# A three-layer graph network on one core: end-node distances on ScalarE, scales of node tiles 8 to 15 found together

## The chip, the cores and the metric

The kernel runs on one core of a Trainium2 chip. Its engines have instruction queues of their own: TensorE (PE in the profile; PEld is its weight load), VectorE (DVE), ScalarE (ACT), GpSimd (POOL) and SyncE (SP, which here only issues DMAs). The metric is the device time of one execution in microseconds (us); the median of several runs is compared.

## The reference

2500 nodes with 256 features each, 80000 edges sorted by their end node `dst`. Each node row is normalized, put through a relu, and three edge convolutions follow; all four states go through one final product, which is added to the input.

```python
def _edge_conv(x, src, dst, W, b):
    xi = x[dst]
    xj = x[src]
    m = jnp.concatenate([xi, xj - xi], axis=-1) @ W + b
    s = jax.ops.segment_sum(m, dst, num_segments=N)
    cnt = jax.ops.segment_sum(jnp.ones((dst.shape[0],), m.dtype), dst, num_segments=N)
    return s / jnp.maximum(cnt, 1.0)[:, None]
...
h = jnp.maximum(_layernorm(x, axis=-1), 0.0)
xs = [h]
for W, b in ((W0, b0), (W1, b1), (W2, b2)):
    h = jax.nn.relu(_edge_conv(h, src, dst, W, b))
    xs.append(h)
return x + jnp.concatenate(xs, axis=-1) @ Wf + bf
```

## The kernel before

The sums over edges are done as matrix products with a matrix of edge counts between nodes. The kernel builds that matrix itself, in the first layer, and keeps a copy in DRAM for the other two. The nodes are 20 tiles of 128 (10 pairs q of two tiles each). The end nodes are cut into 417 windows of 6 nodes; 128 windows make a stretch group i, and there are four of them (0 to 3, the last with 33 windows).

What happens before about 62 us is called the head here. It has two strands of work.

**The nodes.** For each pair q: statistics `st` (line 681 on), for a group of pairs at a time the scales: `spread` adds the epsilon (`rs`, VectorE), `roots` takes the square root (ScalarE), `scales` makes the reciprocal and the offset `off` (VectorE), lines 693 to 702. Then `normalize` applies them (GpSimd for q of 2 and more, otherwise VectorE and ScalarE), `turn` transposes on TensorE, `take_turned` copies with a relu on ScalarE, and `product` makes the first layer's node product `pz` (and the final product's part). ScalarE and VectorE split the product in a high and a low part, `zh` and `zl`.

**The edges.** TensorE, ScalarE and VectorE find where in the edge list each window's edges begin (`count_half`, `search`: the numbers `start_i`). GpSimd then gathers 256 edges for each window, one window on each of the 128 partitions: `ed` from `dst`, then `es` from `src` (`get_edges`, line 584; the last group from `longer`, a copy of the edge list with an end piece). `key_parts` (line 596) makes from them `lo_i`, the low 7 bits of the source, and `away`, how far the end node lies behind the number just under the window's first node, or 0. A second instruction sets the latter half of `away` to 0 where it is small. `key_low` and `key_high` turn them into the keys `km` and `kn`; `key_turn` transposes these on TensorE, `key_copy` copies them out. `compare` (VectorE) makes the 0/1 matrices `one_m` and `one_n` from the keys, for two blocks of four windows at a time (three buffers); `counts` multiplies them on TensorE into a bank, and `take_counts` copies the bank into the count matrix `a` on ScalarE. `away` is read again later, between 62 and 108 us, for the degrees of the nodes.

Most of the instructions are made through `InOrder` wrappers (line 272), so each engine runs its part of the list exactly in the order in which it was written. For the head that order is a string of short names (line 900 on), performed from left to right: a name is a step, the digits its argument. The steps that matter here, with their engines: `st` statistics (VectorE), `rs` spread (VectorE), `sq` root (ScalarE), `sc` scales (VectorE), `N` normalize, `T` turn (TensorE), `R` take_turned (ScalarE), `Z` and `F` products (TensorE), `H` and `L` the high and low parts (ScalarE, VectorE), `G` copy of the final part (ScalarE), `pk` and `sg` counting in the edge list (TensorE, ScalarE), `se` search (VectorE), `ge` gathers (GpSimd), `ka` key_parts, `km` key_low (ScalarE), `kb` key_high (VectorE), `kt` key_turn (TensorE), `k1` and `k2` key_copy (ScalarE), `B` compare (VectorE), `C` counts (TensorE), `E` take_counts (ScalarE). So `ka2` is key_parts of stretch group 2, and `C5` the counts of block 5. The argument of `rs`, `sq` and `sc` is an index in the list `groups` (line 882).

An engine that has to wait for an operand stops there, and all that is behind it in its queue stops too.

After the head the first layer's big products run, while the rest of the count matrix is built beside them, then the other two layers and the final product.

Of the kernel before, what the change touches and what calls it, by code (L numbers as in the profile page):

```python
# [10 lines left out]
AF = mybir.ActivationFunctionType  # L11
OP = mybir.AluOpType
# [301 lines left out]
def by_windows(ctx: ExitStack, tc: tile.TileContext, x, src, dst, Ws, bs, Wf, bf, out, missing):  # L314
    nc = tc.nc
    PE, DVE, ACT, POOL, SP = nc.tensor, nc.vector, nc.scalar, nc.gpsimd, nc.sync
    PEo, DVEo, POOLo, ACTo, SPo = (InOrder(tc, e) for e in (PE, DVE, POOL, ACT, SP))
# [19 lines left out]
    N1 = NT * (W - SKIP)  # L337
# [10 lines left out]
    Q = NT // 2  # L348
# [34 lines left out]
    away = early.tile([P, WG, CAP], BF16, name="away")  # L383
# [13 lines left out]
    lim = const.tile([P, WG], F32, name="lim")  # L397
    below = const.tile([P, WG], F32, name="below")
# [135 lines left out]
    def limits():  # L534
        DVEo.tensor_copy(lim, lim_i)
        DVEo.tensor_copy(limr, limr_i)
        DVEo.tensor_scalar(below, lim, -1.0, None, op0=OP.add)
        DVEo.tensor_scalar(unlim, lim, -1.0, 0.5, op0=OP.mult, op1=OP.add)
        DVEo.tensor_scalar(after, row_i[:, 0:1], -1.0, float(2 ** 20), op0=OP.is_ge, op1=OP.mult)
        DVEo.tensor_copy(dst_r[:, :MORE], row_i)  # L540
# [55 lines left out]
    def key_parts(i):  # L596
        es, ed = edges[i]
        lo_i = pw.tile([P, CAP], I32, name="lo_i")
        DVEo.tensor_scalar(lo_i, es, P - 1, None, op0=OP.bitwise_and)

        DVEo.tensor_scalar(away[:, i, :], ed, below[:, i:i + 1], 0.0, op0=OP.subtract, op1=OP.max)
        DVEo.scalar_tensor_tensor(away[:, i, P:], away[:, i, P:], float(SKIP + 1), away[:, i, P:],
                                  op0=OP.is_ge, op1=OP.mult)
        parts[i] = [lo_i]
# [169 lines left out]
    def new_a(g):  # L774
        return apools[g % 2].tile([P, NT, GS], F32R, name="a")
# [74 lines left out]
    def layer(l, g, a, own, PE=PE, ACT=ACT):  # L850
# [28 lines left out]

    groups = [(0, 1), (1, 2), (2, 4), (4, 6), (6, 8), (8, Q)]
    a = new_a(0)
    acts = {
        "lim": limits, "first": find_first, "next": find_next, "pick": find_rows,
        "long": lengthen,
        "dstr": lambda: ACTo.copy(dst_r[:, MORE:], dst_i),
        "pk": lambda i: pick_half(i // 10, i % 10), "sg": lambda i: count_half(i // 10, i % 10),
        "se": lambda i: search(*((0, 1), (1, WG))[i]), "ge": get_edges,
        "ka": key_parts, "km": key_low, "kb": key_high, "kt": key_turn,  # L890
        "k1": lambda i: key_copy(i, 0), "k2": lambda i: key_copy(i, 1),
        "io": small_numbers, "ws": lambda: DVEo.tensor_sub(ws[0][0], ws[0][0], ws[0][1]),
# [6 lines left out]
    }  # L899
    order = """  # L900
        long warm8 lim io first next dstr st0 rs0 sq0 pick sc0 warm7 N0 pk00 sg00 pk01 st1 T0 pk11 R0 sg01 st4 rs1 sq1 Z0 pk30 se0
        sg11 sc1 pk20 N1 st5 sg30 ge0 T1 st6 R1 rs3 F0 sg20 pk21 sq3 st7 pk10 H0 F1 rs4 st3 sq4 sc4 G0 st9
        sc3 L0 sg21 N6 pk31 ka0 kb0 Z1 N5 st8 N7 G1 T6 rs5 sg10 sg31 km0 T5 se1 kt0 R6 H1 st2 F6 sq5 sc5 k10 k20
        rs2 Z6 ge1 L1 T7 B0 R5 R7 Z5 B1 C0 B2 ka1 G6 H6 N9 H5 C1 T9 F7 E0 ge2 kb1 R9 sq2 km1 E1 kt1 C2 B3 k21 Z9
        k11 N8 L6 B4 E2 L5 C3 B5 C4 T8 E3 E4 C5 V9 R8 E5 ge3 ka2 H9 sc2 Z7 H7 F8 G7 B6 N3 N2 ka3 km2 T2 R2 km3
        kb2 C6 T3 kb3 B7 L7 kt2 Z2 B8 B9 L9 E6 C7 k22 k12 kt3 H2 N4 E7 B10 k13 k23 Z8 L2 C8 T4 C9 E8
# [478 lines left out]
def gnn_kernel(tc: tile.TileContext, x, src, dst, Ws, bs, Wf, bf, out):  # L1385
    nc = tc.nc
    with tc.tile_pool(name="flag", bufs=1) as flag:
        missing = flag.tile([1, 1], I32, name="missing")
        by_windows(tc, x, src, dst, Ws, bs, Wf, bf, out, missing)
        again = nc.values_load(missing, min_val=0, max_val=1)  # L1390
        with tc.If(again > 0):
            general(tc, x, src, dst, Ws, bs, Wf, bf, out)
# [28 lines left out]
```

## Time and profile before

| | before |
|---|---|
| runs | 478.38, 478.60, 479.85 us; median 478.6 |
| profiled execution | 478.51 us, its span 476.7 us, granted TensorE clock 0.996 |
| TensorE, weight load | 465.9 us busy, 366.5 us |
| VectorE, ScalarE, GpSimd | 375.0, 302.1, 41.6 us busy |

The head in stretches of 12 us (busy time of each engine in it):

| stretch, us | PE | DVE | ACT | POOL |
|---|---|---|---|---|
| 0 to 12 | 9.40 | 10.08 | 6.26 | 3.73 |
| 12 to 24 | 11.47 | 11.68 | 8.33 | 7.47 |
| 24 to 36 | 11.45 | 10.47 | 8.70 | 10.66 |
| 36 to 48 | 11.08 | 11.00 | 7.81 | 2.10 |
| 48 to 60 | 12.00 | 11.47 | 7.10 | 0.00 |

Most rows of this kernel carry the line L282, that of the wrapper which records every operation, so its groups are told apart by the tiles that they write and read. A row `away<-ed,below 128x256 bf16<-128x256 int32` writes `away` from `ed` and `below`. A row's length can overlap the next row's start on the same engine, since instructions are pipelined; the distance from one start to the next is then what it takes of the engine. The four instructions `away<-ed,below` take 0.34 to 0.58 us on VectorE in the page's times, mean 0.46; the four casts `km<-lo_i` of the same shape on ScalarE 0.40.

### The profile page before, as it was taken

The page shows a single profiled execution, that of the slowest core. Times are in us where ns is not written, and L with a number is a line of the kernel's source. Part 1 is how long each engine was busy: PE and PEld are TensorE (multiplying, and loading weights), DVE is VectorE, ACT ScalarE, POOL GpSimd, SP SyncE. Part 2 cuts the span into 40 slices and gives each one's busy share as a digit, 9 for nine tenths or more (in the row PEclk, how much of TensorE's full clock was granted, in tenths as well). Part 3 has the DMA queues.
Part 4 walks back from the last instruction along what each step waited for, and adds up shares of the span by engine and source line. Part 5 has one row for each costly group of instructions (what it writes and reads, how often), then busy time and mean ns, then how long its engine had stood idle before and what let it go on. Part 6 is the DMA issues. An engine that isn't in the chain of part 4 may idle for free.

```text
span 476.7 us, 7301 instructions
## 1 busy us (share of the span) xinstructions
PE 465.9 (98%) x2723; PEld 366.5 (77%) x2723; DVE 375.0 (79%) x687; ACT 302.1 (63%) x527; POOL 41.6 (9%) x66
## 2 busy tenths in 40 slices
PE   7999999999999999999999999999999999999994
PEld 4887888777777778878887877876788788688694
DVE  8988987987788874649987847877899687569785
ACT  5776576664554435067778866874787798497540
POOL 3681015200100101000000000000000000000000
PEclk9999999999999999999999999999999999999998
DMA  9310078990550905522268551110213955220033
GB/s 285 112 53 4 1 156 162 192 214 9 102 118 1 203 16 101 119 89 52 79 188 321 210 174 27 61 43 2 87 43 90 356 185 175 87 88 0 0 98 124
DMA packets 21845, 52.73 MB, mean 111 GB/s; under 512 B 1977, under 2 KB 12170, under 8 KB 21770
## 3 DMA queue, kind: packets, MB, share of 16 engines
q1 hardware_dynamic: 14730, 34.31, 21.2%
q0 software_dynamic: 5856, 16.51, 18.2%
q10 hardware_dynamic: 1216, 1.37, 0.9%
q8 instruction: 23, 0.38, 0.3%
q14 instruction: 20, 0.16, 0.1%
HBM read 36.72 MB, written 16.10 MB: 111 GB/s over the span
## 4 chain that ended last, share of the span: by engine, by line
PE 87%; DVE 7%; DMA 2%; POOL 2%; issue 1%; SPq 0%; DVEq 0%
PE bank L282 85%; PE pz L282 2%; DMA acc<-in_x_dram 1%; DVE st L282 1%; DVE acc L282 1%; POOL acc L282 1%; DVE one_m L282 1%; DVE staged L282 1%; DMA es<-longer,start_i 1%; POOL ed L282 1%; DVE one_n L282 1%; DVE zl L282 0%; DVE away L282 0%; DVE mv L282 0%; POOL es L282 0%
## 5 line engine op out<-in xcount | busy, mean ns | idle before, releaser
L282 ACT CAST block<-staged 128x1008 fp32r<-128x1008 bf16 x120 | 117.8, 1031 | 16.9 <-DVE staged L282 6.3
L282 ACT CAST a<-bank 128x480 fp32r<-128x480 f32 (+1 forms) x105 | 52.9, 565 | 60.7 <-PE bank L282 60.7
L282 PE MATMUL bank<-a,zh 128*128 128x504 f32 (+1 forms) x200 | 84.4, 422 | 0.0
L282 PE MATMUL bank<-block,zh 128*128 128x504 f32 (+1 forms) x200 | 83.8, 419 | 0.0
L282 DVE TENSOR_TENSOR one_m<-iota_m,key_m 128x2048 bf16<-128x2048 bf16 (+2 forms) x55 | 64.3, 1169 | 21.4 <-PE bank L282 21.3
L282 PE MATMUL bank<-a,zl 128*128 128x504 f32 (+1 forms) x200 | 77.9, 389 | 0.0
L282 PE MATMUL bank<-block,zl 128*128 128x504 f32 (+1 forms) x200 | 77.4, 387 | 0.0
L282 PE MATMUL bank<-block,sh 128*128 128x504 f32 x160 | 69.1, 432 | 0.0
L282 PE MATMUL bank<-block,staged 128*128 128x512 f32 (+1 forms) x312 | 66.5, 365 | 0.3 <-DVE staged L282 0.3
L282 PE MATMUL bank<-block,sl 128*128 128x504 f32 x160 | 62.7, 392 | 0.0
L282 PEld LDWEIGHTS bank<-block,staged 128*128 128x128 f32 x312 | 52.5, 188 | 10.7 <-issue 0.7
L282 DVE TENSOR_TENSOR one_n<-iota_n,key_n 128x960 bf16<-128x960 bf16 (+2 forms) x110 | 55.5, 545 | 0.0
L282 DVE TENSOR_TENSOR block<-staged 128x1008 fp32r<-128x1008 bf16 x40 | 46.9, 1205 | 5.5 <-PE bank L282 4.3
L282 PEld LDWEIGHTS <-one_m 128*128 128x128 bf16 x834 | 39.1, 98 | 11.2 <-issue 7.2
L282 PEld LDWEIGHTS bank<-a,zh 128*128 128x128 f32 x200 | 37.8, 189 | 10.7 <-issue 2.6
L282 PEld LDWEIGHTS bank<-block,zh 128*128 128x128 f32 x200 | 37.6, 188 | 10.8 <-issue 2.5
L282 PEld LDWEIGHTS bank<-block,zl 128*128 128x128 f32 x200 | 37.6, 188 | 10.5 <-issue 3.2
L282 PE MATMUL bank<-one_n,one_m 128*128 128x120 bf16 x834 | 44.5, 209 | 1.1 <-DVE one_n L282 1.0
L282 PEld LDWEIGHTS bank<-a,zl 128*128 128x128 f32 x200 | 37.8, 189 | 8.9 <-issue 2.6
L282 DVE TENSOR_TENSOR staged<-staged 128x1008 bf16<-128x1008 bf16 x40 | 27.1, 679 | 17.3 <-ACT block L282 16.9
L282 PE MATMUL pz<-wbf,hT 128*128 128x256 f32 x160 | 38.6, 387 | 0.7 <-DMA wbf<-in_L_gnn_Wf_dram 0.4
L282 PEld LDWEIGHTS bank<-block,sh 128*128 128x128 f32 x160 | 30.1, 188 | 10.4 <-issue 3.5
(155 smaller groups left out, 591.1 us busy)
## 6 DMA issues: line engine op xcount, KB each, us to landing
staged<-a_dram SPq DMA_DIRECT2D x52, 504.0 KB, 4.0
a_dram<-a POOLq DMA_DIRECT2D x20, 630.0 KB, 8.6
out_dram<-acc SPq DMA_DIRECT2D x17, 128.0 KB, 1.8
acc<-in_x_dram POOLq DMA_DIRECT2D x3, 640.0 KB, 13.1
wbf<-in_L_gnn_Wf_dram SPq DMA_DIRECT2D x4, 256.0 KB, 6.9
acc<-in_x_dram SPq DMA_DIRECT2D x1, 896.0 KB, 9.4
acc<-in_x_dram ACTq DMA_DIRECT2D x1, 768.0 KB, 6.9
wbf<-in_L_gnn_W_dram SPq DMA_DIRECT2D x3, 256.0 KB
```

Source lines behind the costliest of these rows:

```text
L282: return self.tc.keep_in_program_order(call(*args, **kwargs))
```

## The change

The distance `away` is made by one ScalarE instruction, relu(`ed` + `below`), in place of one VectorE instruction, max(`ed` - `below`, 0); `below` has the opposite sign for it. The masking of the latter half stays on VectorE. In `groups`, the pairs 4, 5 and 6, 7 become one entry, so the scales of their tiles 8 to 15 are made in one step; its `rs` and `sq` stand at the place that those of the pairs 6, 7 had, and one step each of `rs`, `sq` and `sc` is gone. The entry after it has the index 4 in place of 5.

```diff
     def limits():
...
-        DVEo.tensor_scalar(below, lim, -1.0, None, op0=OP.add)
+        DVEo.tensor_scalar(below, lim, -1.0, 1.0, op0=OP.mult, op1=OP.add)
...
     def key_parts(i):
...
-        DVEo.tensor_scalar(away[:, i, :], ed, below[:, i:i + 1], 0.0, op0=OP.subtract, op1=OP.max)
+        ACTo.activation(away[:, i, :], ed, AF.Relu, bias=below[:, i:i + 1])
         DVEo.scalar_tensor_tensor(away[:, i, P:], away[:, i, P:], float(SKIP + 1), away[:, i, P:],
                                   op0=OP.is_ge, op1=OP.mult)
...
-    groups = [(0, 1), (1, 2), (2, 4), (4, 6), (6, 8), (8, Q)]
+    groups = [(0, 1), (1, 2), (2, 4), (4, 8), (8, Q)]
...
-        sg11 sc1 pk20 N1 st5 sg30 ge0 T1 st6 R1 rs3 F0 sg20 pk21 sq3 st7 pk10 H0 F1 rs4 st3 sq4 sc4 G0 st9
-        sc3 L0 sg21 N6 pk31 ka0 kb0 Z1 N5 st8 N7 G1 T6 rs5 sg10 sg31 km0 T5 se1 kt0 R6 H1 st2 F6 sq5 sc5 k10 k20
+        sg11 sc1 pk20 N1 st5 sg30 ge0 T1 st6 R1 F0 sg20 pk21 st7 pk10 H0 F1 rs3 st3 sq3 sc3 G0 st9
+        L0 sg21 N6 pk31 ka0 kb0 Z1 N5 st8 N7 G1 T6 rs4 sg10 sg31 km0 T5 se1 kt0 R6 H1 st2 F6 sq4 sc4 k10 k20
```

## The prediction

> **What bounds the kernel now.** I read the page first: TensorE is busy nearly all of the span, and the table of waits shows it waiting hardly at all after 62 us (0.3 us, for a staged block). So only the head can give or cost time, and only through moments in which TensorE waits there.
>
> ```profile
> PE 465.9 (98%) x2723; PEld 366.5 (77%) x2723; DVE 375.0 (79%) x687; ACT 302.1 (63%) x527; POOL 41.6 (9%) x66
> ```
>
> Next the chain of waits (start, length, what), which shows what carries the head:
>
> ```profile
> 16.91 0.34 DVE lo_i L282
> 17.25 0.50 DVE away L282
> ...
> 33.37 3.43 DMA es<-longer,start_i
> ...
> 36.90 0.29 DVE lo_i L282
> 37.19 0.50 DVE away L282
> ...
> 47.26 0.49 DVE one_n L282
> 47.75 0.04 issue
> 47.80 0.81 PE bank L282 x15
> ```
>
> VectorE carries it from the first statistics on, GpSimd and its last gather (`es` of stretch group 3) for some 13 us, VectorE again to 47.75; from 47.80 it is TensorE, without a break to the end of the head. Two of the four `away` instructions that the change removes stand on this chain. What TensorE loses shows in its own timeline (start, length; in brackets the idle time before and its releaser):
>
> ```profile
> 32.85 0.23 PE L282 MATMUL bank<-one_n,one_m 128*128 128x120 bf16 x1 [0.38 <-DVE one_n L282]
> 33.25 0.46 PE L282 MATMUL bank<-one_n,one_m 128*128 128x80 bf16 x7 [0.17 <-DVE one_n L282]
> 33.55 3.69 PE L282 MATMUL pz<-wbf,hT 128*128 128x256 f32 x16
> 37.08 0.60 PE L282 MATMUL turned<-shift,acc 128*128 128x128 f32 x4
> ...
> 38.96 0.29 PE L282 MATMUL bank<-ident_b,kn 128*128 128x128 bf16 x2 [0.35 <-DVE kn L282]
> 39.08 1.95 PE L282 MATMUL pz<-wbf,hT 128*128 128x256 f32 x8
> 41.33 0.23 PE L282 MATMUL bank<-one_n,one_m 128*128 128x120 bf16 x1 [0.30 <-DVE one_n L282]
> 41.73 0.46 PE L282 MATMUL bank<-one_n,one_m 128*128 128x80 bf16 x7 [0.17 <-DVE one_n L282]
> ```
>
> These are C5, the products Z7 and F8, T2, the turning kt2 of the keys, Z2 and C7. The named idle times sum to 1.4 us; a further 0.4 us or so follows before 47.80 (C11). By starts of one kind of work (C5 could start 32.3, when T8 is issued) the loss is about 0.9 at C5, 0.6 at kt2, 0.5 at C7. About 2 us is all that a faster VectorE can give, 0.4% of the time.
>
> **The groups edit, costed at nothing.** Gone are one `rs` add (0.07 of VectorE's time), one square root on ScalarE (0.11 to the next start), one reciprocal and one `off` (15.87 to 16.29: 0.33 with their gaps): 0.4 us on VectorE before 16.9. But the `lo_i` at 16.91 needs `es` of group 0: that gather is issued at 12.59 and lands 4.3 later, at 16.89. In before, the subtraction `zl` ends at 16.90, so the landing is hidden to the last 0.02; in after VectorE comes at 16.5 and waits until 16.9. The start of that gather (POOL, behind `start_i` at 10.64) is not touched. Moving the root later costs nothing: it follows H0 on ScalarE, ends near 14.45 as the old second root did (14.32 + 0.23), before VectorE wants it at 14.7. Node group N6 on GpSimd waits for the same reciprocal as before (15.19). Folding the sign into `below` changes no count.
>
> **The `away` edit: what VectorE saves.** Four instructions go. From start to the next start they take 0.50 (17.25), 0.37 (26.47 to 26.84), 0.38 (33.65) and 0.53 (37.19 to 37.72). What must come in time is ScalarE's replacement.
>
> *Its price.* No row of before has Relu of integers with a bias. Nearest from below: the cast `km<-lo_i`, same shape and types, 0.40. From above: Relu over `away`, 128x256 with a bias operand, 0.50. The Trainium skill (ScalarE: Activation LUTs, What ACT_TABLE_LOAD costs) gives 280 ns + 0.833 ns an element with such a bias, which for 256 is an estimate of 0.49; I take 0.50, 0.40 from one start to the next. The same page (Rules for kernel authors) speaks against the edit: relu and add belong on VectorE. By that rule four instructions of 0.46 mean are exchanged for four of 0.50: 0.2 us lost if both engines counted alike. By the rows, ScalarE has gaps and VectorE none from 8.4 to 34.6, so the sum is kept by place. A table load has no reason: Relu and Sqrt already alternate here behind the one load at 1.69.
>
> *Place 0.* ScalarE reaches it at 16.16, after the read of the last count, and then sat idle 0.91 before G1 at 17.17, waiting for TensorE. `ed` landed at 11.10 + 4.8 = 15.9. So it ends at 16.66, before `lo_i` ends at 17.25: nothing waits, and VectorE gains 0.50. `se1` then comes at 19.6; its last count is read at 18.92.
>
> *Place 1.* ScalarE comes at 24.82, behind R7; `ed` lands at 21.0 + 2.8 = 23.8 or earlier. G6, H6 shift by 0.40, of which the 0.16 idle and the overlap before H5 absorb all but 0.1; then E0 and R9 have 0.1. TensorE sees none. VectorE's gain is 0.87 by B3 (27.71 becomes 26.84).
>
> *Place 2: here the edit adds a real wait.* On ScalarE it stands behind E5, and E5 waits for C5 on TensorE. C5 now starts at 32.3 and ends 32.85; R8 (32.60) lets E5 start at 33.09; `away` runs 33.55 to 34.05. VectorE would have come at 32.8 and stands still until 34.09; its masking ran at 34.03 before. So the 0.87 is lost again at this point. Behind it wait `sc2`, then N3 and N2 on GpSimd (34.71, released by `off`; nodes 4 and 5 ready at 36.9 as before), and T2 on TensorE. TensorE, 0.9 early out of C5, idles some 0.7 at T2; from T2's second half at 37.05 it is 0.25 early, and reaches kt2 at 38.1 and Z2 at 38.3 if the keys are there.
>
> *Place 3: what the gain rests on.* VectorE was idle 2.29 before 36.90, for the last gather; it decides again. GpSimd's timeline, with its two slow gathers:
>
> ```profile
> 27.94 1.82 POOL L282 DMA_INDIRECT es<-in_src_dram,start_i  x1 [0.30 <-issue]
> 31.05 2.02 POOL L282 DMA_INDIRECT ed<-longer,start_i  x1 [0.16 <-issue]
> 34.71 3.40 POOL L282 TENSOR_SCALAR acc<-acc,rs,off 128x256 f32<-128x256 f32 x6 [0.37 <-DVE off L282]
> ```
>
> The first two started inside a `one_m` of VectorE (begun 27.71 and 31.01), and end 0.92 after it gives way to `one_n` (28.84, 32.15); undisturbed gathers take 0.96. The Trainium skill (SBUF — State Buffer, which ops grab the shared pair) says that a two-input VectorE operation contends with GpSimd's reads but infers that it leaves descriptor generation alone; by that inference GpSimd would be early only by its start, 0.50 (`start_i` at 20.74 to 20.24). By the rows it is tied to `one_m`, hence early by 0.87: N8 at 28.9, ed 30.2, `es` 32.5, landing 35.94 instead of 36.80. I take the rows. ScalarE's `away` runs at 35.6 (H9, H7, G7 before it), ready at 36.1; `ed` is there at 34.6. Then `lo_i` 36.04, masking 36.35 instead of 37.72: 0.86 + 0.51 = 1.37 early. All of VectorE to 47.75 is busy and follows; kn2 is ready at 37.5, before kt2. C7: TensorE 40.1, VectorE 40.35 (41.73 before); C11 at 46.4 for 47.80. Past it TensorE alone decides, so the shift reaches the end.
>
> **Sum.** The profiled execution took 478.51 (span 476.7 and 1.8 around it): 478.51 - 1.37 = 477.1. The median of the runs is 0.1 above it: 477.2. With the lower end of the gather's gain, 0.50 + 0.51 = 1.0: 477.6. Upper end: if the last `ed` slips ahead of B5's `one_m`, `es` lands near 35.0, and ScalarE's `away` (36.1) and TensorE at C7 (40.1) limit: 1.6, and with C11's rest gone 2.0: 476.6.
>
> **Rivals.** *Hidden:* the last gather lands as late as ever (its latency varied from 2.8 to 4.3 for `es`, and place 2 pins N2); then only the 0.51 of place 3 remains, 478.1, or nothing, 478.6, if it also comes late on ScalarE. For it: the place 0 cover of 0.02 shows how landings rule. Against: GpSimd has no other reason to be late.
>
> *Slower:* the wait at place 2 is paid in full. ScalarE's `away` stands behind E5, E5 behind C5, C5 behind B5 on VectorE; every us that it is late moves `sc2`, N2, T2, `ka3` and B7. Its price is that lateness less the slack: it costs from 1.6 us later than I worked out (kt3, behind C7, is then back at its 42.02), and over 0.3% from 3.0 us, 480.1. For it: this loop passes through four queues in order, and VectorE's B7 stands behind it. Against: C5's ones, the bank and E5 all come early.
>
> *More:* the `ed` slip above with C11 gone, 476.6; what speaks against is that both B5 and `ed` move by the same amount.
>
> **Chances.** Forecast (1.0 to 1.6 off) 0.58, hidden 0.20, slower 0.14, more 0.08. About 0.3%, 1.4 us, is what a measurement of this kernel can tell from no change, and the forecast lies across that line: 0.32 of it beyond. Faster 0.32 + 0.08 = 0.40; same 0.26 + 0.20 = 0.46; slower 0.14. The range takes in the upper end with a little more, and the hidden case with the runs' scatter above it: 476.3 to 479.0; the forecast's own is 476.9 to 477.6.
>
> **What would show it.** Right: VectorE idle some 0.4 before the first `lo_i`; ACTIVATE `away<-ed` four times near 0.5; masking at 17.3, 26.0, about 34.1 and about 36.4; C5 at 32.3; T2 waiting for GpSimd near 37; the first unbroken C11 at 46.4. Wrong: a gather that lands after 36.5, masking of group 2 after 34.5, or a gain of the head that is given back past 62 us.

## The result and the profile after

| | before | after |
|---|---|---|
| median of 16 runs | 478.95 us | 477.88 us |
| lowest to highest | 478.24 to 479.85 | 477.40 to 479.37 |
| profiled execution, span | 478.51, 476.7 | 477.85, 476.0 |
| head's end at C11 | 47.80 | 46.81 |
| first big product of the layer | 61.90 | 60.91 |

The ratio is 0.9981, 95% interval 0.9973 to 0.9989: about 1 us, 0.2%, less than the 0.3% that the prediction took as the least change it could tell, though the interval leaves 1 out. Forecast was 477.2. The gain is made before C11 and kept: from the first big product to the end of TensorE's last it is 408.85 us before and 408.84 after (408.81 to 408.86 in all the experiments below). What follows TensorE's end scatters: 5.95 us before, 6.21 after.

The page's first line after the change: engine, busy us, share of the span, instructions.

```profile
PE 465.9 (98%) x2723; PEld 366.2 (77%) x2723; DVE 373.3 (78%) x680; ACT 303.2 (64%) x530; POOL 43.4 (9%) x66
```

Seven VectorE instructions are gone (4 of `away`, 3 of the groups) and ScalarE has three more (4 come, one root goes). GpSimd does the same 66 instructions in 1.8 us more, which will matter below.

VectorE's timeline of after (start, length, operation; in brackets the idle time before and its releaser), first at the four places of `away`, then onward from the last:

```profile
17.08 0.38 DVE L282 TENSOR_SCALAR lo_i<-es 128x256 int32<-128x256 int32 x1 [0.58 <-DMA es<-in_src_dram,start_i]
...
34.27 0.29 DVE L282 SCALAR_TENSOR_TENSOR away<-away 128x128 bf16<-128x128 bf16 x1 [1.61 <-ACT away L282]
...
35.76 0.42 DVE L282 TENSOR_SCALAR lo_i<-es 128x256 int32<-128x256 int32 x1 [0.92 <-DMA es<-longer,start_i]
36.35 0.39 DVE L282 SCALAR_TENSOR_TENSOR away<-away 128x128 bf16<-128x128 bf16 x1 [0.17 <-ACT away L282]
...
36.98 0.58 DVE L282 SCALAR_TENSOR_TENSOR kn<-away,es 128x256 bf16<-128x256 bf16 x1
...
37.80 0.58 DVE L282 SCALAR_TENSOR_TENSOR kn<-away,hi_i 128x256 bf16<-128x256 bf16 x1
...
38.30 1.21 DVE L282 TENSOR_TENSOR one_m<-iota_m,key_m 128x2048 bf16<-128x2048 bf16 x1
39.44 1.25 DVE L282 TENSOR_TENSOR one_n<-iota_n,key_n 128x960 bf16<-128x960 bf16 x2
40.61 0.68 DVE L282 TENSOR_TENSOR zl<-pz,zh 128x512 fp32r<-128x512 f32 x1
```

The first line is the groups edit: VectorE comes 0.4 early and stands 0.58 until `es` of group 0 has landed, which happens 0.17 later than in before. The second is the new wait: the masking of group 2 stands 1.61 for ScalarE. The third and fourth are the gain: the last gather has landed when `lo_i` starts at 35.76 in place of 36.90, and the masking starts at 36.35, not 37.72, which is 1.37 earlier. The two `kn` and B7's `one_n` in the last lines show where 0.4 of that goes: in before they took 0.42, 0.42 and 1.05. The same rows of before:

```profile
37.72 0.52 DVE L282 SCALAR_TENSOR_TENSOR away<-away 128x128 bf16<-128x128 bf16 x1
...
38.48 0.42 DVE L282 SCALAR_TENSOR_TENSOR kn<-away,es 128x256 bf16<-128x256 bf16 x1
...
39.14 0.42 DVE L282 SCALAR_TENSOR_TENSOR kn<-away,hi_i 128x256 bf16<-128x256 bf16 x1
39.48 1.22 DVE L282 TENSOR_TENSOR one_m<-iota_m,key_m 128x2048 bf16<-128x2048 bf16 x1
40.62 1.05 DVE L282 TENSOR_TENSOR one_n<-iota_n,key_n 128x960 bf16<-128x960 bf16 x2
41.59 0.68 DVE L282 TENSOR_TENSOR zl<-pz,zh 128x512 fp32r<-128x512 f32 x1
```

GpSimd's timeline of after:

```profile
27.20 1.49 POOL L282 DMA_INDIRECT es<-in_src_dram,start_i  x1 [0.30 <-issue]
...
29.98 2.02 POOL L282 DMA_INDIRECT ed<-longer,start_i  x1 [0.16 <-issue]
32.30 0.96 POOL L282 DMA_INDIRECT es<-longer,start_i  x1 [0.30 <-issue]
34.95 5.40 POOL L282 TENSOR_SCALAR acc<-acc,rs,off 128x256 f32<-128x256 f32 x6 [1.68 <-DVE off L282]
```

The last gather is issued at 32.30, not 33.37. Then GpSimd stands 1.68 for `off`, since `sc2` is queued behind the waiting masking on VectorE. Its six normalizing instructions start 0.24 later than before and take 5.40 in place of 3.40: they now run beside VectorE's `kn` and B7. Most of the 2.0 is in the last of the six, which begins at 38.09, meets `one_m`, and takes 2.25 where the last of before took 0.58.

TensorE's timeline of after:

```profile
36.66 0.44 PE L282 MATMUL turned<-shift,acc 128*128 128x128 f32 x2
37.34 0.44 PE L282 MATMUL turned<-shift,acc 128*128 128x128 f32 x2 [0.25 <-POOL acc L282]
...
38.55 0.28 PE L282 MATMUL bank<-ident_b,kn 128*128 128x128 bf16 x2
38.66 1.95 PE L282 MATMUL pz<-wbf,hT 128*128 128x256 f32 x8
40.44 0.76 PE L282 MATMUL bank<-one_n,one_m 128*128 128x120 bf16 x8
```

T2 waits for GpSimd; kt2 (38.55) and Z2 wait for nothing; C7 at 40.44 waits briefly within its eight instructions. The chain of waits (start, length, what) of after at the head's end:

```profile
35.91 0.41 ACT away L282
...
36.35 0.39 DVE away L282
...
46.28 0.49 DVE one_n L282
46.77 0.04 issue
46.81 0.81 PE bank L282 x15
```

ScalarE's `away` of group 3 has replaced the gather as the piece ahead of the masking; from there VectorE carries the chain to C11 as it did in before.

### The profile page after: what moved, and what is told of

It reads as the page before. It is cut to its first block, busy times and chain, and to the rows that moved or that the text cites. A ratio compares the mean times of both kernels' runs of the same rounds, so it can differ in the third digit from the quotient of the medians.

```text
span 476.0 us, 7294 instructions
## 1 busy us (share of the span) xinstructions
PE 465.9 (98%) x2723; PEld 366.2 (77%) x2723; DVE 373.3 (78%) x680; ACT 303.2 (64%) x530; POOL 43.4 (9%) x66
## 3 DMA queue, kind: packets, MB, share of 16 engines
q10 hardware_dynamic: 1216, 1.37, 0.9%
## 4 chain that ended last, share of the span: by engine, by line
PE 92%; DVE 4%; DMA 2%; issue 1%; ACT 0%; SPq 0%; DVEq 0%
PE bank L282 86%; PE pz L282 6%; DMA wbf<-in_L_gnn_Wf_dram 2%; DVE acc L282 1%; DVE staged L282 1%; DMA dst_i<-in_dst_dram 1%; DVE one_n L282 1%; DVE one_m L282 0%; PE turned L282 0%; DVE zl L282 0%; DVE kn L282 0%; ACT acc L282 0%; ACT away L282 0%; DVE away L282 0%; SPq L282 0%
## 5 line engine op out<-in xcount | busy, mean ns | idle before, releaser
L282 DVE TENSOR_TENSOR staged<-staged 128x1008 bf16<-128x1008 bf16 x40 | 27.2, 679 | 17.3 <-ACT block L282 16.8
```

The costliest lines, as they stand in the source:

```text
L282: return self.tc.keep_in_program_order(call(*args, **kwargs))
```

## The experiments

Each ratio is against the kernel before on the same chip, with its 95% interval. "First product" is the start of the layer's first big product in the profiled execution: 61.90 in before and 60.91 in after.

**Each half of the change alone.** *away_only*: before, with only the sign of `below` and the `away` edit (shown as an edit of the kernel after).

```diff
-    groups = [(0, 1), (1, 2), (2, 4), (4, 8), (8, Q)]
+    groups = [(0, 1), (1, 2), (2, 4), (4, 6), (6, 8), (8, Q)]
...
-        sg11 sc1 pk20 N1 st5 sg30 ge0 T1 st6 R1 F0 sg20 pk21 st7 pk10 H0 F1 rs3 st3 sq3 sc3 G0 st9
+        sg11 sc1 pk20 N1 st5 sg30 ge0 T1 st6 R1 rs3 F0 sg20 pk21 sq3 st7 pk10 H0 F1 rs4 st3 sq4 sc4 G0 st9
...
```

> Before, with only the four away instructions moved to ScalarE; groups and order as before. Theory (the gain is the away edit's alone; the groups edit's 0.4 us on VectorE are swallowed by the wait for the first es gather): as fast as the whole change, about 1.0 us under before, 477.9, the first lo_i without a long wait, C11's unbroken run at about 46.8. Rival (the groups edit carries part): about 0.4 us slower than the whole change, 478.3.

*groups_only*: the other half, `away` back on VectorE.

```diff
-        DVEo.tensor_scalar(below, lim, -1.0, 1.0, op0=OP.mult, op1=OP.add)
+        DVEo.tensor_scalar(below, lim, -1.0, None, op0=OP.add)
...
-        ACTo.activation(away[:, i, :], ed, AF.Relu, bias=below[:, i:i + 1])
+        DVEo.tensor_scalar(away[:, i, :], ed, below[:, i:i + 1], 0.0, op0=OP.subtract, op1=OP.max)
```

> Before, with only the groups edit and its order; away stays on VectorE. Theory: no difference from before, 478.9 within 0.2 us, VectorE idle some 0.4 us before the first lo_i and C11's unbroken run at 47.8. Rival (the groups edit carries part of the gain): 0.3 to 0.5 us under before, C11 at 47.4.

Measured: away_only 478.16 us, 0.9982 (0.9975 to 0.9989), first product 60.84; groups_only 479.10 us, 1.0003 (0.9995 to 1.0011), first product 62.10. VectorE's timeline of groups_only:

```profile
17.28 0.33 DVE L282 TENSOR_SCALAR lo_i<-es 128x256 int32<-128x256 int32 x1 [0.79 <-DMA es<-in_src_dram,start_i]
```

The 0.4 us that the groups edit takes off VectorE is all spent waiting for the same gather, which in this execution lands 0.38 later than in before. In away_only the same `lo_i` starts at 17.02 with hardly a wait, and all that follows is within 0.2 us of after. The gain is the `away` edit's alone.

**The wait at place 2.** *keep2*: after, with the distance of group 2 alone made by VectorE again. The same kernel was run a second time, *keep2_again*.

```diff
-        ACTo.activation(away[:, i, :], ed, AF.Relu, bias=below[:, i:i + 1])
+        if i == 2:
+            DVEo.tensor_scalar(away[:, i, :], ed, below[:, i:i + 1], 0.0, op0=OP.add, op1=OP.max)
+        else:
+            ACTo.activation(away[:, i, :], ed, AF.Relu, bias=below[:, i:i + 1])
```

> The changed kernel, with away of stretch group 2 alone back on VectorE (as an add of below and a maximum with 0). Theory (the wait for ScalarE at group 2 holds back sc2, by it the normalizing of nodes 4 to 7 on GpSimd and T2 on TensorE; GpSimd's late normalizing then slows kn and B7 of group 3): 0.3 to 0.5 us faster than the changed kernel, 477.4; T2 without a wait at about 36.4, kn at 0.42 instead of 0.58 us, C11 at 46.4. Rival (each away taken from VectorE is worth its length, 0.38 us): 0.4 us slower than the changed kernel, 478.3.

> The kernel with group 2's away on VectorE once more, to narrow its interval beside the changed kernel's. Theory (0.4 us better than the changed kernel): a ratio to before of 0.9965 to 0.9975. Rival (no better than the changed kernel): 0.998 or above.

Measured: 477.50 us, 0.9964 (0.9951 to 0.9977), and 477.68 us, 0.9973 (0.9963 to 0.9984); first product 60.53 and 60.54. Of keep2, GpSimd's timeline and then TensorE's:

```profile
33.71 3.54 POOL L282 TENSOR_SCALAR acc<-acc,rs,off 128x256 f32<-128x256 f32 x6 [0.37 <-DVE off L282]
```

```profile
36.43 0.60 PE L282 MATMUL turned<-shift,acc 128*128 128x128 f32 x4
```

GpSimd normalizes 1.24 earlier than in after and is done in 3.54, T2 waits for nothing, one `kn` takes 0.42 again and B7's `one_n` 1.05. By the first product the wait at place 2 therefore costs 0.38 us (0.37 in the second run); by the times the direction is the same, but the intervals overlap after's, so the times alone don't separate the two.

*late2*: the opposite. Only ScalarE's `away` of group 2 moves, behind H9, H7 and G7 in its queue; the queues of the other engines are as in after.

```diff
-        k11 N8 L6 B4 E2 L5 C3 B5 C4 T8 E3 E4 C5 V9 R8 E5 ge3 ka2 H9 sc2 Z7 H7 F8 G7 B6 N3 N2 ka3 km2 T2 R2 km3
+        k11 N8 L6 B4 E2 L5 C3 B5 C4 T8 E3 E4 C5 V9 R8 E5 ge3 H9 Z7 H7 F8 G7 ka2 sc2 B6 N3 N2 ka3 km2 T2 R2 km3
```

> The changed kernel, with ScalarE's away of stretch group 2 moved behind H9, H7 and G7 in ScalarE's queue; all other queues as in the changed kernel. It makes the masking of group 2 some 2.1 us later without adding work. Theory (there is a slack of about 1.6 us before this wait costs more than the whole change saves, and beyond it every us counts): sc2 at about 36.7, T2's second half at about 39.3, C11 some 1.5 us later than in the changed kernel, 479.4, which is about 0.5 us slower than before. Rival (the last es gather decides, not sc2): no more than 0.9 us slower than the changed kernel (the shift of the masking of group 3), 478.8. Rival (the wait costs its full length): 2.1 us slower, 480.0.

Measured: 484.28 us, 1.0106 (1.0089 to 1.0122), first product 67.31. All the expectations were missed, those of both rivals too. Of late2, the timelines of VectorE, of GpSimd and of TensorE:

```profile
36.32 0.29 DVE L282 SCALAR_TENSOR_TENSOR away<-away 128x128 bf16<-128x128 bf16 x1 [3.68 <-ACT away L282]
```

```profile
37.00 7.43 POOL L282 TENSOR_SCALAR acc<-acc,rs,off 128x256 f32<-128x256 f32 x6 [3.76 <-DVE off L282]
```

```profile
40.89 1.45 PE L282 MATMUL turned<-shift,acc 128*128 128x128 f32 x4 [4.39 <-POOL acc L282]
...
44.12 3.50 PE L282 MATMUL pz<-wbf,hT 128*128 128x256 f32 x8
...
48.04 1.95 PE L282 MATMUL pz<-wbf,hT 128*128 128x256 f32 x8
```

The masking is 2.05 later than in after, yet T2's second half comes at 41.6, 4.3 later than after's 37.34: the third of GpSimd's six instructions, which T2 needs, begins at 38.58, meets B7's `one_m` (38.79) on VectorE and takes 2.25. (In after it was the sixth, for which nothing near waits.) Then eight instructions of one kind take 3.50, and four microseconds later 1.95. The reason is in the table by stages (stretch; its length; busy us of PE, PEld, DVE, ACT, POOL with the instructions in brackets; the granted clock; the DMA share and GB/s):

```profile
30.00:36.00 6.00, 6.00 (x50) 5.38 (x49) 2.64 (x6) 4.60 (x11) 2.94 (x2) 1.00 0.16 44
36.00:41.00 5.00, 0.61 (x4) 0.21 (x3) 4.58 (x12) 0.98 (x3) 4.00 (x4) 0.94 0.00 0
41.00:46.00 5.00, 4.92 (x25) 4.04 (x26) 3.75 (x7) 2.42 (x5) 3.43 (x3) 0.50 0.01 3
46.00:48.00 2.00, 2.00 (x17) 1.61 (x16) 0.00 (x0) 0.34 (x1) 0.00 (x0) 0.69 0.00 0
```

The granted TensorE clock is 0.50 after the idle time of 4.39, and for the first 6 us of work that follow. From T2's second half to C7 it is 5.8 us in place of 3.1. With 4.3 to there, 2.7 more by the half clock and 0.7 won back before C11 (53.15 for 46.81), late2 is 6.3 behind after: 6.4 by the medians. The Trainium skill (TensorE: Matmul & The Clock Gate, The HAM clock gate) states such a fall to half rate for an idle window of about 3.4 us; the trace agrees, and TensorE's waits of up to 0.5 us between 20 and 60 us in before, after and gather_first_pk left the clock at 1.00.

**Taking the wait away without VectorE.** *sc2_early*: VectorE makes the scales `sc2` ahead of group 2's key parts, so GpSimd no longer waits behind the masking.

```diff
-        ... E5 ge3 ka2 H9 sc2 Z7 ...
+        ... E5 ge3 sc2 ka2 H9 Z7 ...
```

> The changed kernel with sc2 moved ahead of ka2 on VectorE (and with it nothing else: the same instructions, ScalarE's and GpSimd's queues unchanged). Theory (what the wait at group 2 costs, it costs by holding back sc2): the wait at the masking stays 1.6 us long, but off is ready near 32.8, GpSimd goes on without a wait after its last gather, T2 has no wait; as fast as the kernel that keeps group 2's away on VectorE, 477.5, 0.4 us under the changed kernel, C11's unbroken run at 46.3. Rival (the wait costs by VectorE's own lost time): as slow as the changed kernel, 477.9.

*sc2_aw3*: the same, with each ScalarE `away` made a step of its own (`aw`), and that of group 3 ahead of H7.

```diff
+    def key_away(i):
+        ACTo.activation(away[:, i, :], edges[i][1], AF.Relu, bias=below[:, i:i + 1])
...
-        ACTo.activation(away[:, i, :], ed, AF.Relu, bias=below[:, i:i + 1])
...
-        ... E5 ge3 ka2 H9 sc2 Z7 H7 ...
+        ... E5 ge3 sc2 aw2 ka2 H9 aw3 Z7 H7 ...
```

> As with sc2 ahead of ka2, and ScalarE's away of group 3 moved ahead of H7 (right behind H9). Theory (with sc2 out of the way the masking of group 3 waits 0.2 to 0.3 us for ScalarE, so this is the next cover): masking of group 3 at 36.1 instead of 36.4 and 0.2 us faster than sc2 alone, 477.3, if TensorE does not limit. Rival (the last gather's landing alone decides): no difference.

Measured: 478.04 us, 0.9977 (0.9969 to 0.9985), first product 60.76; and 477.65 us, 0.9966 (0.9953 to 0.9979), first product 61.12. In sc2_early the scales end near 33.2, GpSimd goes on without a wait and T2 at 36.44 too, as expected. But in both profiled executions the `es` and `kn` of group 0, near 18 us, took 0.57 and 0.66 in place of 0.28 and 0.50 beside GpSimd, which made everything behind them 0.45 later from there on. That is as large as the effect that was sought, so their times and first products tell neither case from after. VectorE's timeline of sc2_early tells more:

```profile
34.30 0.32 DVE L282 SCALAR_TENSOR_TENSOR away<-away 128x128 bf16<-128x128 bf16 x1 [0.92 <-ACT away L282]
...
36.86 0.28 DVE L282 TENSOR_SCALAR es<-es 128x256 int32<-128x256 int32 x1
...
39.48 1.05 DVE L282 TENSOR_TENSOR one_n<-iota_n,key_n 128x960 bf16<-128x960 bf16 x2
40.45 0.68 DVE L282 TENSOR_TENSOR zl<-pz,zh 128x512 fp32r<-128x512 f32 x1
```

VectorE still waits for ScalarE at place 2, but GpSimd begins its six instructions at 33.74, and from the `es` row of group 3 to `zl` behind B7 it is 3.59 us. That is what keep2 has too; before has 3.43, and after and away_only, where GpSimd is late, 3.95 and 3.94. (sc2_aw3 has 3.72, of which 0.3 is the slow `es` row itself.) So what VectorE loses behind the masking goes with GpSimd's place, not with the wait itself. In sc2_aw3 the masking of group 3 no longer waits for ScalarE but for the gather (`lo_i` at 36.45).

**When a gather is slow.** *gather_first*: sc2_aw3, with the gathers of group 3 queued ahead of N8 on GpSimd (T8, R8, C6 and T3 reordered to fit). *gather_first_pk*: also `pk21` ahead of F0 on TensorE. From after to the latter, the order alone (the `aw` step is as above):

```diff
-        ... R1 F0 sg20 pk21 st7 ...
+        ... R1 sg20 pk21 F0 st7 ...
...
-        k11 N8 L6 B4 E2 L5 C3 B5 C4 T8 E3 E4 C5 V9 R8 E5 ge3 ka2 H9 sc2 Z7 H7 F8 G7 B6 N3 N2 ka3 km2 T2 R2 km3
-        kb2 C6 T3 kb3 B7 L7 kt2 Z2 ...
+        k11 ge3 N8 L6 B4 E2 L5 C3 B5 C4 E3 E4 C5 V9 E5 sc2 N3 N2 aw2 ka2 H9 aw3 Z7 T8 R8 H7 C6 T3 F8 G7 B6 ka3 km2 T2 R2 km3
+        kb2 kb3 B7 L7 kt2 Z2 ...
```

> As the one before, and the gathers of group 3 issued ahead of the normalizing N8 on GpSimd, with T8, R8, C6 and T3 set later or earlier so that TensorE has work. Theory (a gather that starts before a one_m is not held by it, one that starts inside ends 0.9 us after the one_m): ed of group 3 starts at 28.9 and takes 1.0 instead of 2.0 us, es lands near 34.5 instead of 35.7; VectorE is at B7 a good us earlier, TensorE has no wait at C7 and C11: 0.6 to 0.8 us faster than the one before, 476.6. Rival (TensorE is the bound by then): 0.2 us or less.

> As the one before, and one count of the edge search (pk21, 0.2 us of TensorE) ahead of F0 instead of behind it, into TensorE's 0.6 us wait for F0's weights at 13.3. Theory (from 13.3 to the end TensorE has hardly a wait left): 0.2 us faster than the one before, 476.4. Rival (VectorE and the gathers still decide somewhere): no difference.

Measured: 478.14 us, 0.9979 (0.9973 to 0.9986), first product 60.73; and 477.75 us, 0.9974 (0.9963 to 0.9985), first product 60.65. Of gather_first_pk, the timelines of GpSimd, VectorE and TensorE:

```profile
29.02 0.95 POOL L282 DMA_INDIRECT ed<-longer,start_i  x1 [0.30 <-issue]
30.27 1.73 POOL L282 DMA_INDIRECT es<-longer,start_i  x1 [0.30 <-issue]
```

```profile
29.97 1.21 DVE L282 TENSOR_TENSOR one_m<-iota_m,key_m 128x2048 bf16<-128x2048 bf16 x1
```

```profile
32.41 0.51 PE L282 MATMUL bank<-one_n,one_m 128*128 128x120 bf16 x8 [0.29 <-ACT a L282]
...
38.97 1.99 PE L282 MATMUL pz<-wbf,hT 128*128 128x256 f32 x8 [0.47 <-ACT hT L282]
```

The first gather is over (29.97) when `one_m` begins, and takes 0.95; the second starts within it and ends 0.90 after `one_m` gives way (31.10 to 32.00). (That a gather begun ahead of a `one_m` is not held while it overlaps it shows elsewhere: in after the `es` begun at 21.57 takes 0.95 though a `one_m` runs beside it from 21.83.) So `lo_i` of group 3 starts at 34.39, and VectorE is 1.5 us ahead at B7 (36.78 for 38.30). The time gains nothing clear of it: TensorE now waits for ScalarE, 0.29 at C5 and 0.47 at Z2 (there ScalarE had itself waited 1.26 for T2, late in TensorE's new order), and reaches C7 at 40.80. gather_first's rival, that TensorE is the bound by then, held; moving `pk21` brought the first product forward by 0.08, too little to tell from none.

**A version built on this.** *best*: gather_first_pk, with TensorE's and ScalarE's order fitted to it: Z7 ahead of C5, T2 ahead of F8 and T3 behind it, N2 ahead of N3, ScalarE's `away` of group 2 ahead of E3, E5 behind C5 and E6 ahead of R2.

```diff
-        k11 ge3 N8 L6 B4 E2 L5 C3 B5 C4 E3 E4 C5 V9 E5 sc2 N3 N2 aw2 ka2 H9 aw3 Z7 T8 R8 H7 C6 T3 F8 G7 B6 ka3 km2 T2 R2 km3
-        kb2 kb3 B7 L7 kt2 Z2 B8 B9 L9 E6 C7 ...
+        k11 ge3 N8 L6 B4 E2 L5 aw2 C3 B5 C4 E3 E4 Z7 V9 sc2 N2 N3 ka2 H9 aw3 H7 C5 E5 T8 R8 C6 T2 F8 G7 ka3 km2 E6 R2 km3
+        B6 kb2 kb3 B7 L7 T3 kt2 Z2 B8 B9 L9 C7 ...
```

> As the last of the gather-first kernels (gathers of group 3 ahead of N8, pk21 ahead of F0), with its TensorE order mended: Z7 ahead of C5, T2 ahead of F8, T3 behind it, N2 ahead of N3 on GpSimd, ScalarE's away of group 2 ahead of E3. Theory (gather-first freed VectorE 1.5 us earlier at B7, but TensorE then waited at C5, F8 and Z2 for banks, T8 and R2 of my own order): no wait of TensorE over 0.2 us between 31 and 47 us, C7 at 39.7 instead of 40.8, layer 0's products from 59.5 instead of 60.7; 1.2 us faster than that kernel, 476.5. Rival (time past the head takes it back, whatever the head gains beyond 1 us): the products from 59.5, but the time at 477.4 or more.

Measured: 476.81 us against 478.9 for before, 0.9960 (0.9946 to 0.9973), near what was expected. TensorE's timeline of best, and a line of its table of waits between 24 and 62 us (who waits for whom; us in total, times, the longest):

```profile
59.48 0.58 PE L282 MATMUL bank<-a,zh 128*128 128x504 f32 x1
```

```profile
PEld pz L282 <- ACT hT L282: 0.2, 1, 0.2
```

The first product is 1.43 earlier than in after and 2.42 earlier than in before, and that 0.2 is all that the table has of TensorE's waits between 24 and 62 us. It is faster than before by its interval; than after by 1.1 us of the medians, with intervals that touch.

## Why the prediction was right, and where it was not

The forecast's mechanism came as written but for what follows the last masking. The time, 477.88, is 0.7 above the forecast and outside the forecast's own 476.9 to 477.6, though inside the whole range. Half of the 0.7 is the level: before itself came out at 478.95 where the prediction had set out from 478.6. Of the gain, 1.4 was forecast and 1.07 measured.

- **The groups edit, costed at nothing**: shown by groups_only, and by the 0.58 that VectorE then waits.
- **The price of `away`** on ScalarE: the group of `away<-ed,below` has 499, 514 and 541 ns (least, median, most), the forecast 0.50. The rule against the edit (the Trainium skill, ScalarE: Activation LUTs, Rules for kernel authors) did not decide: ScalarE had gaps, and in away_only the four moved instructions gained 0.8 us by the times, 1.1 by the first product.
- **The places**: ScalarE came at 16.32, 25.00, 33.70 and 35.80 (forecast 16.16, 24.82, 33.55, 35.6), the masking at 17.38, 25.78, 34.27 and 36.35 (17.3, 26.0, 34.1, 36.35).
- **Place 3, gathers tied to `one_m`**: held. Both slow gathers end 0.92 after their `one_m` gives way (27.77 to 28.69, 31.07 to 32.00), and the last `es` is issued 1.07 earlier, not the 0.50 that the prediction drew from the inference of the Trainium skill (SBUF — State Buffer, which ops grab the shared pair), with which the gathers' rows do not agree. VectorE was ahead by 1.07 at B3, not by 0.87, for at place 0 the masking and `kn` got shorter too (0.27 for 0.52, 0.50 for 0.58). So the gather landed 0.2 sooner than forecast (35.74 for 35.94), ScalarE's `away` came 0.2 later and decided, and that the masking still fell on the forecast 36.35 is luck.
- **The mis-sized term** is what follows the masking: "All of VectorE to 47.75 is busy and follows" carried the 1.37 to C11 unchanged, which gave 46.4 for the measured 46.81. From the masking to B7's `one_m` it is 1.95 in after for 1.76 in before, though the masking itself is shorter; from `one_n` to `zl` 1.17 for 0.97. That is 0.39, and 1.37 less 0.39 is the 0.98 by which the `one_n` just ahead of C11 comes earlier (46.28 for 47.26). The prediction said that GpSimd's N3 and N2 are held behind the wait at place 2 but took into account only who waits for them (T2), not what they then run beside. keep2, in which GpSimd has its old place, has its first product 0.38 earlier, and sc2_early agrees.
- **T2** waited for GpSimd as forecast, but its second half came at 37.34, not 37.05: `off` came 0.24 later than forecast. TensorE's idle times there sum to 0.4, not 0.7. It cost nothing further, for C7 waited for VectorE.
- **The rivals *Hidden* and *More*** did not come. The measured time lies nearer to the hidden case's 478.1 than to 477.2, but its sign, a gather that lands after 36.5, is absent; nor did the last `ed` slip ahead of B5's `one_m`: it started at 29.98, within it.
- **The slower rival** did not come, but its price was wrong, and the chance rested on it. It held that the wait costs from 1.6 us later than worked out, microsecond for microsecond. In late2 the masking came 2.2 later than worked out, for which that gives 0.6 over before; late2 was 1.06%, some 5 us, over it. Missing were GpSimd's collision with B7 (2.25 for one tile) and the half clock after the idle time. The place was closer to a loss than the prediction showed.

Not settled: why `es` and `kn` of group 0 ran slow in the profiles of sc2_early and sc2_aw3, and whether keep2 is faster than after in time.

## What to carry to other kernels

An instruction that is moved to an engine with gaps pays by the place at which that engine reaches it, not by its own length, so work out each place and then follow what its wait releases later: the released work may now run beside something that it slows. A wait put on the bounding engine's feeders need not cost in proportion: here one of 1.61 us cost 0.38, and 2.05 more on top of it cost another 6.3, through a collision on GpSimd and an idle time that halved TensorE's clock. And an edit that brought one strand 1.5 us forward gave next to nothing until the order on the engine that bounds was fitted to it.

## What the runs showed of the hardware

- An indirect gather of 128x256 integers (groups 1 to 3) takes GpSimd 0.95 to 1.08 us when it begins ahead of a `one_m` (128x1024 or 128x2048, VectorE), even if that starts beside it, and 1.5 to 2.0 when it begins within one, ending 0.9 after that gives way. Those last 0.9 run beside `one_n`, the same operation (128x960, 27.77 to 28.82 in after), without further delay. Why a gather is held by the `one_m` that it meets and not by the `one_n` that follows stays open.
- GpSimd and VectorE slow each other in both directions: six normalizing instructions took 3.40 (before), 5.40 (after) or 7.43 us (late2) by what ran beside them; VectorE's `kn` took 0.42, 0.50, 0.58 or 0.66.
- The last stretch, from the end of the last addition on VectorE to the end of the span, when TensorE has ended, took from 5.1 (before) to 6.1 us (sc2_early, gather_first_pk). A difference of some tenths between single profiled executions is within that scatter; the first product's start is steadier ground.
